# Self-attention over four images in exact-split fp32: biases as one row, later images' projection in pairs of units

## Chip, cores and metric

The kernel runs on one core of a Trainium2 chip. The metric is device time in microseconds (us) of one launch. Each engine of the core runs its own queue in order: PE (TensorE; its weight loads are shown as PEld), ACT (ScalarE), DVE (VectorE), POOL (GpSimd) and SP (SyncE, which here only issues DMAs).

## The reference

Input x has shape (4, 64, 64, 256). Per image (N = 4096 positions, C = 256):

```python
q = x @ Wq + bq                 # (N, 128)
k = x @ Wk + bk                 # (N, 128)
v = x @ Wv + bv                 # (N, 256)
pq, pk, pv = q.reshape(128, N), k.reshape(128, N), v.reshape(256, N)
energy = pq.T @ pk              # (N, N)
attention = softmax(energy, axis=-1)
out = gamma * (pv @ attention.T) + x
```

The reshapes reinterpret memory, they do not transpose.

## The kernel before, in words

**Split arithmetic.** A value y is carried as three "forms" in the fp32r format: h (most of y), l (the rest, y - h) and d (h and l mixed with other weights). A product of two values is then three matmul passes (form numbers f = 0, 1, 2). ACT writes h; DVE writes l and d, each from y and h. `split` (L151) does this for x and v, `qk_forms` (L261) for q and k, `upper` (L341, ACT) and `halves` (L348, DVE) for the exponentials. With `two` set, `split` lets DVE write l and POOL write d (L159).

**Work units.** Projection of an image is cut into 16 units of 256 positions. A unit is: load x (`load_x`, SP), four PE transposes into a PSUM bank (`transposed`, L214), the three forms of x (`x_forms`), q and k by 8 + 4 matmuls of 256 columns (`products` with w = 0, L239), v by as many (w = 1); a bias added in PSUM between the first pass and the others (`seed_qk` on DVE, `seed_v` on ACT); forms of q, k and v, and stores of these to DRAM by SP (`store`, L292). Image 0 is projected first, in a phase of its own (about the first 70 us), with v's forms written straight into `vall` in SBUF. Images 1 to 3 are projected while the image before them is attended; their v comes back through DRAM (`load_v`, POOL).

**Attention.** There are 512 steps n (128 an image). A step handles 256 keys (t = n mod 16) for 512 queries; 16 steps are a group. In a step PE does, in this order: `cross(n+2)`, 2 matmuls (form 2 of k and q; ACT then scales the PSUM tile e, L322); `attend(n, 0)`, 6 matmuls of 512 columns for the first 128 channels: 2 with h and 2 with l into bank a0, 2 with d into b0; `energy(n+2)`, 4 matmuls onto e, after which ACT takes exp (L339); a piece of projection; and `attend(n, 1)`, 6 matmuls for the other channels (banks a1, b1). That is 18 matmuls of 512 columns. ACT's `upper(n+2)` writes h of the new exponentials. DVE's `halves(n+1)` adds them to the running sum (L356), then writes l (L370) and d (L372).

**The turn.** After step t = 15 the four banks a0, b0, a1, b1 are full. ACT empties a0 and b0 in step t = 15 and a1, b1 in the next step (t = 0) after its exp (`emptied`, L407), which `attend(n, 1)` of step t = 0 waits for; `upper` of the step is put off behind that. ACT also writes zf, h of the group's total (`sum_forms`, L419; DVE writes its l), which PE sums over partitions in step t = 0 (`sums`, z, L431); ACT copies z out (L432), and `finish`, one piece a step, sends 1/z around through DRAM and stores the output.

**Order.** The schedule is manual: each engine runs its instructions in the order in which the Python code emits them, and tiles of one tag share a ring of buffers, so a new tile waits until the last user of its buffer is done. `step(p, engine)` (L522) emits the projection's piece number p on one engine: unit p // 8, stage r = p mod 8. In the loop (L646) p = n - 4 up to n = 15, two pieces a step for n = 16 to 23, then p = n + 4. Two PSUM banks, p0 and p1, are used in turn for x transposed, q and k, v, and z. In image 3's steps (`late`) no projection is left, and a1 and b1 are emptied in step t = 1.

**Biases.** bq and bk are loaded with one copy for each of the 128 partitions (L131, L132), bv into two columns by POOL (L128); ACT and POOL scale them (L588, L587).

## Time and profile before

| | |
|---|---|
| median of 3 runs | 2358.5 us (2358.07 to 2359.53) |
| profiled execution | 2360.35 us, its span 2358.6 us |
| DMA | 413.82 MB, mean 175 GB/s |
| ACT's 128 x 512 emptying (L407) | 0.69 to 0.70 us each, 124 of them |
| DVE 128 x 1024 (L356, L370, L372) | 1.22 us each, 480 of each |
| DVE 128 x 512 form of q, k (L271), x and v (L163) | 0.68 us each |
| v store (vf) of a unit, k load | 768 KB by SP, 384 KB by POOL (3.7 us to landing) |

The span runs from the first to the last instruction. Busy time of PE is modelled from pipelined matmuls, so the distance between starts says more than a duration. In a waits line stand the engine and line that waited, what released it, the total in us, how often, and the longest. In a timeline stand the start, the duration, engine, line, operation, output<-inputs, shapes, a count, and in brackets idle time before and its releaser.

### The profile page before, as it was taken

How to read it: one execution, taken by the hardware profiler on the slowest of the kernel's cores; microseconds unless marked ns; L12 is line 12 of the kernel's file. 1: busy time of each engine (PE TensorE's matmuls, PEld its weight loads, DVE VectorE, ACT ScalarE, POOL GpSimd, SP SyncE). 2: the span in 40 equal slices, each digit the busy share in tenths (PEclk: the TensorE clock that was granted, in tenths of full speed). 3: DMA queues.
4: the chain of work that ended last, by engine and by line, in shares of the span. 5: the costliest groups of instructions: out<-in, count | busy, mean ns of one | idle time of the engine just before them, and what ended most of it. 6: DMA issues, size and time to landing. Idle time of an engine off the chain costs nothing.

```text
span 2358.6 us, 31984 instructions
## 1 busy us (share of the span) xinstructions
PE 2340.2 (99%) x11104; PEld 1955.8 (83%) x11104; DVE 2129.4 (90%) x2095; ACT 1870.8 (79%) x3074; POOL 397.7 (17%) x671
## 2 busy tenths in 40 slices
PE   8999999999999999999999999999999999999998
PEld 8888888888888888888888888888888888888886
DVE  7989999989999899998999999999989888888887
ACT  6778778888788887888877888778887777888875
POOL 6211111111211111111121111111112111111110
PEclk9999999999999999999999999999999999999999
DMA  8556665556975566556597555665559554454443
GB/s 259 175 157 171 186 165 165 164 158 178 295 247 175 148 172 186 159 162 157 165 340 226 159 167 152 184 169 162 168 154 353 158 135 120 123 130 117 131 130 96
DMA packets 179110, 413.82 MB, mean 175 GB/s; under 512 B 26079, under 2 KB 76767, under 8 KB 178942
## 3 DMA queue, kind: packets, MB, share of 16 engines
q0 software_dynamic: 94208, 280.54, 45.2%
q1 hardware_dynamic: 83902, 130.77, 15.5%
q8 instruction: 91, 1.49, 0.3%
q14 instruction: 77, 0.63, 0.1%
q10 hardware_dynamic: 832, 0.39, 0.1%
HBM read 306.64 MB, written 104.98 MB: 175 GB/s over the span
## 4 chain that ended last, share of the span: by engine, by line
PE 96%; ACT 1%; DVE 1%; POOL 1%; issue 0%; DMA 0%; SPq 0%; DVEq 0%; ACTq 0%; POOLq 0%
PE a L393 39%; PE e L336 20%; PE b L393 19%; PE e L321 10%; PE qv L239 7%; PE xt L214 1%; PE z L431 1%; ACT x L339 0%; ACT o L407 0%; DMA xs<-in_x_dram 0%; POOL xf L159 0%; ACT e L322 0%; POOL v L159 0%; DVE f L271 0%; DVE ld L372 0%
## 5 line engine op out<-in xcount | busy, mean ns | idle before, releaser
L339 ACT ACTIVATE x<-e 128x512 f32<-128x512 f32 x960 | 522.3, 596 | 296.6 <-PE e L336 290.3
L356 DVE TENSOR_TENSOR s<-s,x 128x1024 f32<-128x1024 f32 x480 | 586.3, 1222 | 94.1 <-ACT x L339 91.5
L370 DVE TENSOR_TENSOR ld<-x,h 128x1024 fp32r<-128x1024 f32 x480 | 585.9, 1221 | 88.2 <-ACT h L345 57.9
L393 PE MATMUL a<-h,v 128*128 128x512 f32 x2048 | 641.0, 394 | 0.0
L393 PE MATMUL b<-ld,v 128*128 128x512 f32 x2048 | 631.6, 390 | 1.7 <-DVE ld L372 1.7
L322 ACT ACTIVATE e<-e 128x512 f32<-128x512 f32 x1024 | 546.7, 572 | 108.9 <-PE e L321 108.6
L393 PE MATMUL a<-ld,v 128*128 128x512 f32 x2048 | 632.7, 390 | 0.0
L308 POOL DMA_DIRECT2D k<-kf x512 | 272.7, 533 | 1903.4 <-PE e L336 1797.5
L372 DVE SCALAR_TENSOR_TENSOR ld<-h,x 128x1024 fp32r<-128x1024 f32 x480 | 585.6, 1220 | 0.0
L336 PE MATMUL e<-q,k 128*128 128x512 f32 x2048 | 548.8, 390 | 1.1
L345 ACT ACTIVATE h<-x 128x1024 fp32r<-128x1024 f32 x480 | 510.3, 1063 | 13.3
L393 PEld LDWEIGHTS b<-ld,v 128*128 128x128 f32 x2048 | 384.2, 188 | 84.7 <-DVE ld L372 1.5
L393 PEld LDWEIGHTS a<-ld,v 128*128 128x128 f32 x2048 | 384.5, 188 | 83.1
L336 PEld LDWEIGHTS e<-q,k 128*128 128x128 f32 x2048 | 383.1, 188 | 84.4 <-ACT e L322 6.0
L393 PEld LDWEIGHTS a<-h,v 128*128 128x128 f32 x2048 | 368.6, 189 | 69.4 <-ACT o L407 7.3
L321 PE MATMUL e<-q,k 128*128 128x512 f32 x1024 | 316.0, 390 | 0.0
L321 PEld LDWEIGHTS e<-q,k 128*128 128x128 f32 x1024 | 191.8, 188 | 40.7 <-issue 0.2
L239 PEld LDWEIGHTS qv<-wf,xf 128*128 128x128 f32 x768 | 107.5, 192 | 10.4 <-POOL xf L159 1.3
L239 PE MATMUL qv<-wf,xf 128*128 128x256 f32 x768 | 112.9, 286 | 1.8 <-DVE xf L163 0.8
L239 PEld LDWEIGHTS qv<-xf,wf 128*128 128x128 f32 x768 | 106.3, 191 | 8.8 <-ACT s L432 0.7
L239 PE MATMUL qv<-xf,wf 128*128 128x256 f32 x768 | 110.5, 283 | 0.5 <-ACT s L432 0.3
L271 DVE SCALAR_TENSOR_TENSOR f<-f,qv 128x512 fp32r<-128x512 f32 x128 | 85.7, 680 | 3.6 <-ACT f L268 2.1
(78 smaller groups left out, 1021.6 us busy)
## 6 DMA issues: line engine op xcount, KB each, us to landing
k<-kf POOLq DMA_DIRECT2D x512, 384.0 KB, 3.7
vf<-vf SPq DMA_DIRECT2D x48, 768.0 KB
v<-vf POOLq DMA_DIRECT2D x48, 768.0 KB, 7.8
kf<-f SPq DMA_DIRECT2D x128, 192.0 KB
qd<-f SPq DMA_DIRECT2D x128, 192.0 KB
q<-qd POOLq DMA_DIRECT2D x31, 768.0 KB, 4.7
o<-in_x_dram POOLq DMA_DIRECT2D x31, 512.0 KB, 7.3
out_dram<-o SPq DMA_DIRECT2D x31, 512.0 KB
```

What stands on the lines that cost most here:

```text
L239: nc.tensor.matmul(to[:, s, :], left, right.rearrange("p s a -> p (s a)") if w else right, start=(f == 2 and s == k == 0), stop=(f == 1 an ...
L271: nc.vector.scalar_tensor_tensor(f[:, :, :, j, :], h.bitcast(F32), s, y, ALU.mult, op)
L308: nc.gpsimd.dma_start(t, kf[b, u % NU])
L321: nc.tensor.matmul(e, *forms(n, i, 2), start=True, stop=False, skip_group_check=True)
L322: nc.scalar.mul(e, e, -REST)
L336: nc.tensor.matmul(e, *forms(n, i, f), start=False, stop=(f == 1), skip_group_check=True)
L339: nc.scalar.activation(x[:, i, :], e, AF.Exp, scale=(1.0 + E) ** 3 / E)
L345: nc.scalar.activation(h, units[n], AF.Identity, scale=UPPER)
L356: nc.vector.tensor_tensor(s, s, x, ALU.add)
L370: nc.vector.tensor_tensor(l, x, h.bitcast(F32), ALU.subtract)
L372: nc.vector.scalar_tensor_tensor(d, h.bitcast(F32), 1.0 + E, x, ALU.mult, ALU.subtract)
L393: nc.tensor.matmul(to, vall[:, t, f, i, j * P : (j + 1) * P], units[n][f][:, i, :], start=(t == 0 and i == 0 and f != 1), stop=(t == NU - ...
```

## The change

- **Biases.** bq, bk and bv are loaded as one row of 512 on one partition, on ACT's queue. PE spreads bq and bk over the partitions (a matmul of a column of ones with the row) and turns bv into two columns (two matmuls with a single 1); ACT scales from PSUM.
- **Image 0.** Unit 1's forms are all DVE's; unit 2 is transposed later, after v of unit 0 has begun. v's forms of units 14 and 15 are DVE's alone.
- **Later images by pairs.** A piece sequence now has 16 stages for two units. Both units are transposed together; x's forms h and l lie side by side for both units, d in the buffer in which x was loaded (tag "xd"). q and k stay 256 columns wide. v is made for both units at once by 512-column matmuls, one half of the channels at a time (`products_v`), with one seed for each half. A half's forms go to DRAM in two stores. `vall` and vf have the order half, form instead of form, half.
- **One step behind.** p = n - 3 + (n > 6) + (n > 17), with two pieces in steps 6 and 17 alone; from n = 18 on stage 15, which emits nothing, falls on t = 0.
- **Turn.** In steps t = 0 (not in image 3) `attend(n+1, 0)` with h and l is emitted ahead of `attend(n, 1)`; in t = 1 only its d is left between `cross` and `energy`.
- **Buffers.** zf takes a buffer of the ring "pf" (the forms of q, k and v, two buffers); the row of 1/z goes into the second half of o.

```diff
-        vall = qkv.tile([P, NU, 3, 2, C], F32R, tag="v", name="v")
+        vall = qkv.tile([P, NU, 2, 3, C], F32R, tag="v", name="v")
...
-        nc.scalar.dma_start(bias[:, :C2], bq.partition_broadcast(P))
-        nc.scalar.dma_start(bias[:, C2:], bk.partition_broadcast(P))
+        nc.scalar.dma_start(rows[:, :C2], bq.unsqueeze(0))
+        nc.scalar.dma_start(rows[:, C2:C], bk.unsqueeze(0))
+        nc.scalar.dma_start(rows[:, C:], bv.unsqueeze(0))
...
+            pair = work.tile([P, 2, 2, XB], F32, tag="xd", name=f"x_{b}_{i}", bufs=1)
+            for u in range(2):
+                nc.sync.dma_start(pair[:, u], xv[b, i + u])
+                loads["x", b, i + u] = pair[:, u]
...
-            yield from split(f[:, 0], f[:, 1], f[:, 2], y, b == 0 and i > 0)
+            yield from split(*f, y, b == 0 and i > 1)
...
+        def products_v(b, i, eh, fs):
+
+            xf = now["xf"]
+            if fs[0] == 2:
+                units["v", b, i, eh] = bank(f"v{eh}_{b}_{i}", [P, 2, C], b, 1)
+            to = units["v", b, i, eh]
+            for f in fs:
+                for k in range(KC):
+                    nc.tensor.matmul(
+                        to.rearrange("p u c -> p (u c)"),
+                        wf[:, 1, f, k, eh * P : (eh + 1) * P],
+                        xf[f][:, k].rearrange("p u s a -> p (u s a)"),
...
+        def seed_v_pair(b, i, eh):
+            y = units["v", b, i, eh]
+            nc.scalar.activation(y, y, AF.Identity, bias=bvs[:, eh : eh + 1], scale=REST)
...
+            yield from split(*(vall[:, i, :, f] for f in range(3)), y, i < NI - 2)
+
+        def v_pair_forms(b, i, eh):
+            y = units.pop(("v", b, i, eh))
+            f = work.tile([P, 2, 3, C], F32R, tag="pf", name=f"vf{eh}_{b}_{i}")
+            yield from split(*(f[:, :, j] for j in range(3)), y)
+            for u in range(2):
+                stores.append((vf[b, i + u][:, eh], f[:, u]))
...
-            f = work.tile([P, 2, NB], F32R, tag="r", name=f"zf_{n // NU}", bufs=1)
+            f = work.tile([P, 2, NB], F32R, tag="pf", name=f"zf_{n // NU}")
...
-            r = work.tile([P, NB], F32, tag="r", name=f"r_{n}", bufs=1)
+            r = o[:, 1, 0]
...
+            if engine == "pe":
                 if r == 0:
                     transposed(b, i)
+                    transposed(b, i + 1)
+                elif r == 5:
                     products(b, i, 0, (2,))
+                    products(b, i + 1, 0, (2,))
+                elif r == 6:
                     products(b, i, 0, (0, 1))
+                    products(b, i + 1, 0, (0, 1))
+                elif r in (9, 11):
+                    products_v(b, i, r // 11, (2,))
+                elif r in (10, 12):
+                    products_v(b, i, r // 12, (0, 1))
+            elif engine == "act":
+                if r in (1, 2):
+                    begin(("x", r - 1), x_forms(b, i + r - 1))
+                elif r in (7, 8):
+                    begin(("qk", r - 7), qk_forms(b, i + r - 7))
+                elif r in (10, 12):
+                    seed_v_pair(b, i, r // 12)
+                    if r == 12:
+                        load_x(b + (i + 2) // NI, (i + 2) % NI)
+                elif r in (11, 13):
+                    begin(("v", r // 13), v_pair_forms(b, i, r // 13))
+            else:
+                if 1 <= r <= 4:
+                    next(made["x", (r - 1) // 2])
                 elif r == 5:
+                    seed_qk(b, i)
+                    seed_qk(b, i + 1)
+                elif 7 <= r <= 10:
+                    next(made["qk", (r - 7) // 2])
...
+                elif 11 <= r <= 14:
+                    next(made["v", (r - 11) // 2])
...
-            p = n - 4 if n < 16 else 2 * n - 20 if n < 24 else n + 4
+            p = n - 3 + (n > 6) + (n > 17)
             step(p, "act")
-            if not final:
+            late = n >= (B - 1) * STEPS
+            if t == 1 and n > 1 and not late:
+                attend(n, 0, (2,))
+            elif not final:
                 attend(n, 0)
...
+            if t == 0 and n and not late:
+                attend(n + 1, 0, (0, 1))
             attend(n, 1)
...
-            if 16 <= n < 24:
+            if n in (6, 17):
                 for engine in ("act", "pe", "dve"):
                     step(p + 1, engine)
```

More of the change, by code (lines that the diff above doesn't have):

```diff
@@ L126 @@
         nc.gpsimd.memset(zs, 1.0)
-        for eh in range(KC):
-            nc.gpsimd.dma_start(bvs[:, eh : eh + 1], bv[eh * P : (eh + 1) * P].unsqueeze(1))
+        rows = work.tile([P, 2, XB], F32, tag="pf", name="rows")[:1]
+        rows = rows.rearrange("p s f -> p (s f)")
         make_identity(nc, ident)
         nc.vector.tensor_scalar(ones_r, zs.to_broadcast([P, P]), 1.0, None, ALU.mult)
-        nc.scalar.dma_start(bias[:, :C2], bq.partition_broadcast(P))
-        nc.scalar.dma_start(bias[:, C2:], bk.partition_broadcast(P))
+        nc.scalar.dma_start(rows[:, :C2], bq.unsqueeze(0))
+        nc.scalar.dma_start(rows[:, C2:C], bk.unsqueeze(0))
+        nc.scalar.dma_start(rows[:, C:], bv.unsqueeze(0))
         nc.scalar.activation(zs, zs, AF.Exp)
@@ L183, in image @@
                 kf[b, t] = dram.tile([P, 2, 3, P], F32, tag=f"kf{t}", name=f"kf_{b}_{t}")
-                vf[b, t] = dram.tile([P, 3, 2, C], F32, tag=f"vf{t}", name=f"vf_{b}_{t}")
+                vf[b, t] = dram.tile([P, 2, 3, C], F32, tag=f"vf{t}", name=f"vf_{b}_{t}")
         def bank(name, shape, b, ring):
@@ L198, in load_x @@
         def load_x(b, i):
-            if i >= NI:
+            if b == B or i >= NI:
                 return
@@ L202, in load_x @@
                 t = xs4[:, i % 4]
-            else:
-                t = work.tile([P, 2, XB], F32, tag="xin", name=f"x_{b}_{i}", bufs=1)
-            if b or i:
-                nc.sync.dma_start(t, xv[b, i])
-            loads["x", b, i] = t
+                if i:
+                    nc.sync.dma_start(t, xv[b, i])
+                loads["x", b, i] = t
+                return
+            pair = work.tile([P, 2, 2, XB], F32, tag="xd", name=f"x_{b}_{i}", bufs=1)
+            for u in range(2):
+                nc.sync.dma_start(pair[:, u], xv[b, i + u])
+                loads["x", b, i + u] = pair[:, u]
         def transposed(b, i):
@@ L218, in x_forms @@
             y = units.pop(("xt", b, i))
-            if b == 0 and i % 3 < 2:
-                f = ppool.tile([P, 3, KC, 2, P], F32R, tag="ld", name=f"xf_{b}_{i}")
-            else:
-                f = work.tile([P, 3, KC, 2, P], F32R, tag="xf", name=f"xf_{b}_{i}", bufs=1)
+            if b == 0:
+                if i % 3 < 2:
+                    f = ppool.tile([P, 3, KC, 2, P], F32R, tag="ld", name=f"xf_{b}_{i}")
+                else:
+                    f = work.tile([P, 4, KC, 2, P], F32R, tag="xf", name=f"xf_{b}_{i}", bufs=1)
+                f = [f[:, j] for j in range(3)]
+            else:
+                if i % 2 == 0:
+                    shape = [P, 2, KC, 2, 2, P]
+                    f = work.tile(shape, F32R, tag="xf", name=f"xf_{b}_{i}", bufs=1)
+                    d = work.tile([P, *shape[2:]], F32R, tag="xd", name=f"xd_{b}_{i}", bufs=1)
+                    now["xf"] = [f[:, 0], f[:, 1], d]
+                f = [y_[:, :, i % 2] for y_ in now["xf"]]
             units["xf", b, i] = f
-            yield from split(f[:, 0], f[:, 1], f[:, 2], y, b == 0 and i > 0)
+            yield from split(*f, y, b == 0 and i > 1)
         def products(b, i, w, fs):
@@ L235, in products @@
                         if w:
-                            left, right = wf[:, 1, f, k, s * P : (s + 1) * P], xf[:, f, k]
+                            left, right = wf[:, 1, f, k, s * P : (s + 1) * P], xf[f][:, k]
                         else:
-                            left, right = xf[:, f, k, s, :], wf[:, 0, f, k]
+                            left, right = xf[f][:, k, s, :], wf[:, 0, f, k]
                         nc.tensor.matmul(
@@ L246, in products @@
                         )
+        def products_v(b, i, eh, fs):
[9 more added lines that the diff above has]
+                        xf[f][:, k].rearrange("p u s a -> p (u s a)"),
+                        start=(f == 2 and k == 0),
+                        stop=(f == 1 and k == KC - 1),
+                        skip_group_check=True,
+                    )
         def seed_qk(b, i):
@@ L252, in seed_qk, with seed_v @@
             )
-        def seed_v(b, i):
-            y = units[1, b, i]
+        def seed_v(i):
+            y = units[1, 0, i]
             for eh in range(KC):
@@ L277, in qk_forms, with v_forms @@
                 stores.append((qd[b, i // NJ + NG // 2 * s][:, i % NJ], f[:, s, 0]))
-        def v_forms(b, i):
-            y = units.pop((1, b, i))
-            units.pop(("xf", b, i))
-            if b == 0:
-                f = vall[:, i]
-            else:
-                f = work.tile([P, 3, 2, C], F32R, tag="pf", name=f"vf_{b}_{i}")
-            yield from split(f[:, 0], f[:, 1], f[:, 2], y, b == 0)
-            if b:
-                stores.append((vf[b, i], f))
+        def v_forms(i):
+            y = units.pop((1, 0, i))
+            units.pop(("xf", 0, i))
+            yield from split(*(vall[:, i, :, f] for f in range(3)), y, i < NI - 2)
[5 more added lines that the diff above has]
+                stores.append((vf[b, i + u][:, eh], f[:, u]))
         def store():
@@ L394, in attend @@
                         to,
-                        vall[:, t, f, i, j * P : (j + 1) * P],
+                        vall[:, t, i, f, j * P : (j + 1) * P],
                         units[n][f][:, i, :],
@@ L471, in finish_last @@
             S = now["sum"][:, 0, :]
-            f = work.tile([P, 2, NB], F32R, tag="r", name="zf_last", bufs=1)
+            f = work.tile([P, 2, NB], F32R, tag="pf", name="zf_last")
             nc.scalar.activation(f[:, 0, :], S, AF.Identity, scale=UPPER)
@@ L517, in finish_last @@
             nc.sync.dma_start(og[b, g][:, 1], xr[:, 1, :])
-        R = STEPS // NI
+        R = 2 * STEPS // NI
         def step(n, engine):
@@ L527, in step, with begin @@
             i, r = divmod(u, R)
-            b += 1
+            b, i = b + 1, 2 * i
+            if b >= B:
+                return
             made = now["made"]
-            if engine == "pe" and b < B:
+            def begin(key, pieces):
+                made[key] = pieces
+                next(pieces)
+            if engine == "pe":
                 if r == 0:
                     transposed(b, i)
-                elif r == 3:
+                    transposed(b, i + 1)
+                elif r == 5:
@@ L534, in step @@
                     products(b, i, 0, (2,))
-                elif r == 4:
+                    products(b, i + 1, 0, (2,))
+                elif r == 6:
                     products(b, i, 0, (0, 1))
-                elif r == 5:
-                    products(b, i, 1, (2,))
-                elif r == 6:
-                    products(b, i, 1, (0, 1))
-            elif engine == "act" and b < B:
-                if r == 1:
-                    made["x"] = x_forms(b, i)
-                    next(made["x"])
-                    load_x(b, i + 1)
-                elif r == 5:
-                    made["qk"] = qk_forms(b, i)
-                    next(made["qk"])
-                elif r == 6:
-                    seed_v(b, i)
-                elif r == 7:
-                    made["v"] = v_forms(b, i)
-                    next(made["v"])
-            elif engine == "dve":
-                if r == 0 and "v" in made:
-                    for _ in made.pop("v"):
-                        pass
-                if b < B:
-                    if r in (1, 2):
-                        next(made["x"])
-                    elif r == 3:
-                        seed_qk(b, i)
-                    elif r == 5:
-                        next(made["qk"])
-                    elif r == 6:
-                        for _ in made.pop("qk"):
-                            pass
-                    elif r == 7:
-                        next(made["v"])
@@ new lines, in step @@
+                    products(b, i + 1, 0, (0, 1))
[14 more added lines that the diff above has]
+                    begin(("v", r // 13), v_pair_forms(b, i, r // 13))
+            else:
+                if 1 <= r <= 4:
+                    next(made["x", (r - 1) // 2])
+                elif r == 5:
+                    seed_qk(b, i)
+                    seed_qk(b, i + 1)
+                elif 7 <= r <= 10:
+                    next(made["qk", (r - 7) // 2])
+                    if r % 2 == 0:
+                        next(made["qk", (r - 7) // 2], None)
+                elif 11 <= r <= 14:
+                    next(made["v", (r - 11) // 2])
+                    if r % 2 == 0:
+                        next(made["v", (r - 11) // 2], None)
@@ L586 @@
         next(w0)
-        nc.gpsimd.tensor_scalar(bvs, bvs, REST / E, None, ALU.mult)
-        nc.scalar.activation(bias, bias, AF.Identity, scale=REST)
         next(w1)
         products(0, 0, 0, (2,))
+        bb = ps_e.tile([P, KC + C], F32, tag="e", name="bb")
+        nc.tensor.matmul(bb[:, KC:], ones[:1], rows[:, :C], start=True, stop=True)
+        nc.scalar.activation(bias, bb[:, KC:], AF.Identity, scale=REST)
         seed_qk(0, 0)
-        xs = []
-        for i in (1, 2):
-            transposed(0, i)
-            load_x(0, i + 3)
-            xs.append(x_forms(0, i))
-            next(xs[-1])
-        next(xs[0])
+        transposed(0, 1)
+        load_x(0, 4)
+        x1 = x_forms(0, 1)
+        next(x1)
         next(w1)
+        next(x1)
         next(w1)
+        next(x1)
         nc.gpsimd.tensor_scalar(gam1, gam, 1.0 + E, None, ALU.mult)
@@ L607 @@
             if i == 0:
-                products(0, 0, 1, (2,))
-                seed_v(0, 0)
+                for eh in range(KC):
+                    nc.tensor.matmul(
+                        bb[:, eh : eh + 1],
+                        rows[:, C + eh * P : C + (eh + 1) * P],
+                        ones[:1, :1],
+                        start=True,
+                        stop=True,
+                    )
+                nc.scalar.activation(bvs, bb[:, :KC], AF.Identity, scale=REST / E)
+                products(0, 0, 1, (2,))
+                seed_v(0)
+                transposed(0, 2)
+                load_x(0, 5)
+                x2 = x_forms(0, 2)
+                next(x2)
             if i + 1 < NI:
@@ L616 @@
             if i == 0:
-                next(xs[1])
+                next(x2)
             products(0, i, 1, (0, 1))
-            vs = v_forms(0, i)
+            vs = v_forms(i)
             next(vs)
@@ L624 @@
                 products(0, i + 1, 1, (2,))
-                seed_v(0, i + 1)
+                seed_v(i + 1)
             if i + 3 < NI:
@@ L654 @@
                 image(b + 2)
-                load_x(b + 2, 0)
             if n == B * STEPS - 6:
@@ L672 @@
             store()
-            late = n >= (B - 1) * STEPS
             if t == 0 and n:
```

## The prediction

> **What bounds the kernel now.** I read the page first, then the chain that ended last, the waits, and the timeline of single steps. TensorE (PE) is the bound:

> ```profile
> PE 2340.2 (99%) x11104; PEld 1955.8 (83%) x11104; DVE 2129.4 (90%) x2095; ACT 1870.8 (79%) x3074; POOL 397.7 (17%) x671
> ...
> PE 96%; ACT 1%; DVE 1%; POOL 1%; issue 0%; DMA 0%; SPq 0%; DVEq 0%; ACTq 0%; POOLq 0%
> ```

> Busy 99% does not yet say that PE streams without gaps, so I look at spacing. The chain in order of time shows the first matmuls after each group turn (a group is 16 steps; a turn is a step with t = 0):

> ```profile
> 660.54 1.08 PE a L393 x4
> ...
> 733.34 1.08 PE a L393 x4
> ```

> A group takes 72.80 us, and so does every later group that carries projection, to 0.01 us. PE's timeline gives the prices inside it:

> ```profile
> 700.72 0.64 PE L239 MATMUL qv<-xf,wf 128*128 128x256 f32 x4
> 701.20 0.63 PE L393 MATMUL a<-h,v 128*128 128x512 f32 x2
> ...
> 705.30 1.11 PE L239 MATMUL qv<-xf,wf 128*128 128x256 f32 x8
> 706.25 0.63 PE L393 MATMUL a<-h,v 128*128 128x512 f32 x2
> ...
> 714.45 0.60 PE L214 MATMUL xt<-ident,x 128*128 128x128 f32 x4
> ```

> Starts, not durations, are the price. A 512-column matmul follows the last after 0.2269 us, a 256-column one after 0.120 us, a transpose after 0.108 us. Every small block also makes the next few 512-column matmuls a little late; with that a block of four costs 0.498, of eight 0.978, four transposes 0.477 (blocks measured to the eighth matmul behind them). One unit of projection is 0.477 + 2 x 0.498 + 2 x 0.978 = 3.43. A group: 290 x 0.2269 (16 steps of 18 matmuls, and z) + 2 x 3.43 = 72.66. What is left, 0.16, is the turn.

> **Pairs, and v 512 columns wide.** Per pair of units PE now does 8 transposes in a row (0.477 + 4 x 0.108 = 0.909), q and k as a block of 8 and one of 16 (0.978 + 1.938), and v as 12 matmuls of 512 columns in place of 24 of 256 (12 x 0.2269 = 2.723, no small block among the others). Sum 6.548 against 6.856: 0.308 saved, 24 pairs: **-7.4 us**, bounds -8 and -1.1 (the transposes' 0.045 alone). ACT and DVE do the same splits (DVE 0.68 each, starting 0.61 apart); v's seed is two ACT passes of about 0.6 a pair instead of four of 0.45, on an engine with 21% idle. DVE's heaviest step carries 3 x 1.155 + 0.61 + 1.15 = 5.2 us against PE's 4.08, but the steps around it are light, and before had peaks as high without making PE wait.

> [...]

> **The turn.** This is the step that I fear. The waits, then the turn at 729.04 (call it T), PE, ACT and DVE:

> ```profile
> PEld a L393 <- ACT o L407: 7.3, 23, 0.3
> ```
> ```profile
> 729.04 0.62 PE L321 MATMUL e<-q,k 128*128 128x512 f32 x2
> ...
> 731.76 1.12 PE L239 MATMUL qv<-wf,xf 128*128 128x256 f32 x8
> 732.71 0.63 PE L431 MATMUL z<-zf,ones 128*128 128x512 f32 x2
> 733.22 0.73 PE L393 MATMUL a<-h,v 128*128 128x512 f32 x2
> ```
> ```profile
> 729.46 1.07 ACT L322 ACTIVATE e<-e 128x512 f32<-128x512 f32 x2 [0.30 <-PE e L321]
> 730.43 1.06 ACT L345 ACTIVATE h<-x 128x1024 fp32r<-128x1024 f32 x1
> ...
> 734.57 0.56 ACT L432 COPY s<-z 1x512 f32<-1x512 f32 x1
> 735.13 1.07 ACT L322 ACTIVATE e<-e 128x512 f32<-128x512 f32 x2
> ```
> ```profile
> 731.53 1.23 DVE L370 TENSOR_TENSOR ld<-x,h 128x1024 fp32r<-128x1024 f32 x1 [1.78 <-ACT h L345]
> ```

> From T on ACT has no idle until the next step's e. PE waited 0.16 at 733.22 for ACT to empty a's bank, and the block of eight (0.98) covered the rest. In the changed kernel the projection stands one step behind, so the step with t = 0 has no block; z, then h and l of the next step's attend(n+1, 0), stand there instead. Step by step, from T, with the same durations:
> - PE would reach l of step n+1 at 2.72 (energy done) + 0.454 (z) + 0.454 (h) = T + 3.63. DVE ends that l at 731.53 + 1.23, T + 3.72; the step before the turn is shorter now (4.08, not 4.58, no block), so ACT's e starts at T + 0.49 instead of 0.42, and l ends at 3.78. A wait that ends late costs its weight load too: at 733.22 the second matmul came 0.34 after the first, not 0.23, and the load started 0.05 after ACT's end. So l runs from 3.78 + 0.16 = 3.94: 0.31 lost.
> - Then l, attend(n, 1): next step at T' = 3.94 + 0.454 + 1.361 = 5.755. a's bank (free at about 4.2) is no longer waited for.
> - There only d stands between cross and energy, 0.907 after T' instead of 1.81. ACT's e starts at 6.17 by its own chain and by cross (T' + 0.42) alike, and the first ends at 6.76: energy runs from 6.92, not 6.66, and its second half loses 0.04 more.
> The whole loses 0.61 a turn, where before lost 0.16: 0.45 x 23 turns = **+10.4 us**. Bounds: -3.7 (nothing waits) and +17 (ACT's chain 0.3 later still).

> **zf in the ring of the forms ("pf").** At each turn ACT writes zf into the buffer of the pair's first v half, so it waits for that half's two stores, and exp, emptying and e stand behind it on ACT. DVE finishes that half some 3.1 us into step t = 13, SP issues at once, behind the next pair's two loads of x. ACT wants zf 10.5 us into step 13 (4.99 + 4.08 + 1.46), 7.4 us after the issue. The packets of an ordinary vf store of before ended 5.7 us after their issue: in time, with 0.38 us of idle on ACT behind. But in the last group of an image v is loaded too (DMA share 1.0 to 1.1 from 608 to 657 us), and the stores at 642.9, 1225.4 and 1807.5 ended after 10.6, 9.6 and 7.0 us. By these ACT is late by 3.2, 2.2 and 0, less 0.38 each: 4.7 us for three turns; by the ordinary row 0. I take the middle, **+2.3**, bounds 0 and +10 (two smaller stores in place of one, behind more loads). The 48 further store issues (0.55 us each) cost SP nothing, it is mostly idle. POOL's loads of the last v pair wait a little longer for their stores; the k loads behind them have three steps, 12 us, of lead over a landing of 3.7.

> **Image 0's end.** v's d of units 14 and 15 moves from POOL to DVE:

> ```profile
> 70.61 2.31 DVE L372 SCALAR_TENSOR_TENSOR ld<-h,s 128x1024 fp32r<-128x1024 f32 x1
> ```
> ```profile
> 69.64 2.20 POOL L159 TENSOR_TENSOR v<-v 128x512 fp32r<-128x512 f32 x1 [1.49 <-DVE v L156]
> ```

> Side by side both run nearly twice as long as alone (DVE 1.22, POOL 1.3). It comes again at 75.8, and PE waits for this DVE row both times (1.1 and 0.9 us). Without POOL, DVE saves 1.09 and pays 0.61 each time: **-0.9**, bounds -1 and +1.2 (if POOL is not the cause).

> **Double steps.** Before runs two projection steps in each of 16 to 23; at 148.0 PE lost 0.57 there to the copy of z. The changed kernel doubles only 6 and 17: **-0.6**, or 0.

> **The start.** PE stands from 7.6 to 10.55 for the second x; ACT's bias waits until 10.43 for a broadcast row, 128 KB with its partner. One row of 2 KB and a small matmul in PE's idle time take their place; x_1 lands earlier by up to 1 us, the first q and k no longer stand behind unit 2's transposes, and POOL loses a pass, but DVE gets x_1's d and the next wait (POOL until 20.03) is fed by DVE. PE's granted clock is 0.5 between 9.1 and 15.9 us, so nothing is made up there. **-1.0**, bounds -2 and +1 (late rows hold PE's queue). Image 3 has no projection and is unchanged.

> **Sum.** -7.4 + 10.4 + 2.3 - 0.9 - 0.6 - 1.0 = +2.8 us. The profiled execution took 2360.35 (span 2358.6), so it would take 2363.2; the median of the runs is 1.85 lower, 2358.5, and gives **2361.3**. A measurement here can tell about 0.2%, 4.7 us, from no change: 2353.8 to 2363.2 is "the same".

> **Rivals.**
> - *The turn's waits vanish* (faster): l and e come early enough and the 0.16 goes as well: -3.7 in place of +10.4, 2347.2. For it: 0.31 and 0.30 are small against chains of ten instructions. Against: ACT's chain has no gap to give. It decides where l ends before T + 3.47.
> - *zf holds ACT at every turn* (slower): if the two stores take 9 us in ordinary groups as well, 1.2 lost x 20 turns, 2385; with 8.2 us, 0.4 each, 2369. For it: x's loads stand ahead. Against: 5.7 us was steady.
> - *v's pairs save nothing*: if a wide v matmul costs as much as two of 0.120, and switching as much as before, only the transposes' 0.045 a pair is left, -1.1 in place of -7.4: 2367.6. Against: 0.120 and 0.2269 repeat in all groups. [...]

> **How the numbers follow.** Forecast 0.48, range of its own 2355 to 2367: of it 0.03 falls under "faster", 0.33 "same", 0.12 "slower". Waits vanish 0.22, all faster. zf 0.16: 0.03 same, 0.13 slower. No saving 0.06, slower. Small terms at their other bounds 0.08: 0.01, 0.05, 0.02. Faster 0.26, same 0.41, slower 0.33. The range, 2347 to 2371, takes in the first rival and the small end of the second.

> **What would show it.** Right: a group of about 73 us between z's; among the waits PEld for DVE's ld and for ACT's e, some 23 each, and none for ACT o until image 3; DVE's row at 70.6 back at 1.22; v matmuls 0.227 apart. Wrong: groups under 72.4, or zf waiting for vf's DMA outside three turns.

## The result and the profile after

Before took 2358.96 us (median of 6 runs, 2358.07 to 2359.53), the changed kernel 2378.26 us (6 runs, 2373.45 to 2382.86): ratio 1.0081, 95% interval 1.0070 to 1.0092. It is 0.8% slower, and lies 7 us above the top of the range on record. Its profiled execution took 2377.93 us (span 2376.0).

The page of the changed kernel: first the busy times, then the shares of the chain that ended last.

```profile
PE 2353.1 (99%) x10822; PEld 1943.2 (82%) x10822; DVE 2127.3 (90%) x2098; ACT 1853.7 (78%) x3027; POOL 389.4 (16%) x665
...
PE 89%; ACT 5%; DMA 2%; DVE 2%; issue 1%; SPq 0%; POOL 0%; ACTq 0%; DVEq 0%
```

PE is still "busy" for 99%, but the chain tells another story: before, PE alone made 96% of it; now 89%, and DMA holds 2% where it held 0%. DMA on the chain means that somebody on the critical path waits for a transfer. The waits name who (engine and line, what it waited for: us in total, times, longest):

```profile
PEld e L371 <- ACT e L357: 19.9, 62, 0.6
...
PEld a L428 <- DVE ld L405: 10.5, 21, 0.7
PEld e L356 <- ACT x L374: 9.9, 8, 4.2
ACT zf L454 <- DMA vf<-vf: 8.3, 3, 4.8
ACT vf L154 <- DMA qd<-f: 8.2, 5, 2.8
PE e L356 <- ACT x L374: 7.1, 4, 3.8
...
ACT vf L154 <- DMA vf<-vf: 2.1, 1, 2.1
...
PEld a L428 <- ACT o L442: 1.3, 4, 0.4
```

Two families. The small and frequent ones (0.7 and 0.6 at most) are the turn: l and e arrive late, as forecast (of the 62 waits for e, two at each of 23 turns are new; the other 16 stand in image 3, where before has them too). The wait for ACT's emptying of o has shrunk from 23 times to 4, at 146.2, 661.3, 1251.2 and 1838.9 us, each behind one of the large waits. The large and rare ones are new: ACT waits 3 times for a store of v's forms before it may write zf, 5 times for stores of q and k and once for one of v's before it may write a v half, and PE then waits for ACT's exp (x), up to 4.2 us at a time.

The chain in order of time over one ordinary turn shows the first family as a row of pieces:

```profile
733.60 1.09 ACT x L374 x2
734.69 1.16 ACT o L442 x2
735.85 0.97 ACT e L357 x2
736.81 0.98 ACT h L380
737.80 0.02 issue
737.82 1.24 DVE ld L405
739.06 0.04 issue
739.10 1.65 PE a L428 x6
```

ACT makes exp, empties two banks, makes e and h without a pause, DVE makes l, and PE's `a<-ld` starts 0.04 after l's end. Where did the time come from? I measured from z to z (the matmul that sums zf, once in each group), one interval for each group:

```
z to z, us   ordinary groups   last group of image 0   of image 1   the group with image 2's end
before       72.80 to 72.81    72.81                   72.81        79.46
after        72.86 to 72.99    78.29                   79.81        83.53
```

Nineteen ordinary intervals grew by 0.17 each on average, 3.2 us together (seventeen of them take 72.97 to 72.99; the two that follow the long groups 72.94 and 72.86). Two groups grew by 5.5 and 7.0, the third by 4.1 (the third holds more work after than before, see v_not_loaded below). These three, in which v of the next image is loaded, and the first turn are the story. This is ACT and PE in the first of them, changed kernel (start and duration in us, engine, line, what, and in brackets the idle time before it and who ended it):

```profile
643.34 0.60 ACT L154 ACTIVATE vf<-v 128x512 fp32r<-128x512 f32 x1 [2.55 <-DMA qd<-f]
...
659.07 0.63 ACT L454 ACTIVATE zf<-s 128x512 fp32r<-128x512 f32 x1 [3.35 <-DMA vf<-vf]
```
```profile
657.72 0.61 PE L428 MATMUL b<-ld,v 128*128 128x512 f32 x2
660.24 0.98 PE L356 MATMUL e<-q,k 128*128 128x512 f32 x2 [1.91 <-ACT x L374]
661.31 0.73 PE L428 MATMUL a<-h,v 128*128 128x512 f32 x2
661.88 0.77 PE L428 MATMUL a<-ld,v 128*128 128x512 f32 x2
662.44 1.05 PE L428 MATMUL b<-ld,v 128*128 128x512 f32 x2
663.29 1.91 PE L371 MATMUL e<-q,k 128*128 128x512 f32 x4
```

ACT stands 3.35 us at zf; exp stands behind zf, cross behind exp, and PE loses 2.07 at once and 0.61 in the next starts (a "stand" of PE, below, is time that it loses like this to a wait). Then comes something that the prediction had no term for: the block of four at 663.29 takes 1.91 instead of 1.07. The busy times by stretch say why (columns: the stretch, its length, busy time of PE, PEld, DVE, ACT and POOL, then the granted clock, the busy share of the DMA engines, and GB/s):

```profile
640.00:658.00 18.00, 17.51 (x76) 13.61 (x74) 13.76 (x14) 11.71 (x20) 3.86 (x8) 1.00 1.10 400
658.20:660.20 2.00, 0.14 (x1) 0.00 (x0) 0.47 (x1) 1.13 (x3) 0.17 (x1) 1.00 1.07 346
662.20:665.60 3.40, 3.40 (x10) 2.62 (x9) 1.79 (x2) 2.53 (x5) 0.10 (x1) 0.50 0.73 288
665.70:669.00 3.30, 3.30 (x15) 2.46 (x14) 2.27 (x3) 3.19 (x7) 0.86 (x2) 1.00 0.71 211
```

The DMA share is 1.1 while the stores are awaited, PE does next to nothing for 2 us, and behind that the clock is 0.5 for 3.4 us, in which each matmul starts 0.43 after the last. In the next image's last group the stand is 3.91 and the half clock lasts 6.8 us (1249.31 to 1256.14).

### The profile page after: what moved, and what is told of

The parts are those of the page before. It is cut to its first block, busy times and chain, and to the rows that moved or that the text cites. A ratio compares the mean times of both kernels' runs of the same rounds, so it can differ in the third digit from the quotient of the medians.

```text
span 2376.0 us, 31544 instructions
## 1 busy us (share of the span) xinstructions
PE 2353.1 (99%) x10822; PEld 1943.2 (82%) x10822; DVE 2127.3 (90%) x2098; ACT 1853.7 (78%) x3027; POOL 389.4 (16%) x665
## 3 DMA queue, kind: packets, MB, share of 16 engines
q8 instruction: 89, 1.46, 0.3%
## 4 chain that ended last, share of the span: by engine, by line
PE 89%; ACT 5%; DMA 2%; DVE 2%; issue 1%; SPq 0%; POOL 0%; ACTq 0%; DVEq 0%
PE a L428 36%; PE e L371 18%; PE b L428 18%; PE e L356 9%; PE qv L252 5%; PE v L269 2%; ACT x L374 2%; ACT o L442 1%; DVE ld L405 1%; PE xt L218 1%; DMA vf<-vf 1%; DMA qd<-f 1%; ACT e L357 1%; ACT h L380 1%; DVE ld L407 0%
## 5 line engine op out<-in xcount | busy, mean ns | idle before, releaser
L407 DVE SCALAR_TENSOR_TENSOR ld<-h,x 128x1024 fp32r<-128x1024 f32 x480 | 585.8, 1220 | 0.0
L428 PEld LDWEIGHTS a<-ld,v 128*128 128x128 f32 x2048 | 383.0, 188 | 89.9 <-DVE ld L405 10.5
L428 PEld LDWEIGHTS a<-h,v 128*128 128x128 f32 x2048 | 379.6, 188 | 76.1 <-ACT o L442 1.3
L252 PE MATMUL qv<-wf,xf 128*128 128x256 f32 x576 | 79.2, 289 | 1.7 <-POOL xf L160 0.8
L252 PEld LDWEIGHTS qv<-wf,xf 128*128 128x128 f32 x576 | 75.4, 195 | 5.1 <-POOL xf L160 1.0
L164 DVE SCALAR_TENSOR_TENSOR vf<-vf,v 128x512 fp32r<-128x512 f32 x96 | 65.4, 682 | 5.9 <-ACT vf L154 5.8
L405 DVE TENSOR_TENSOR ld<-s,h 128x1024 fp32r<-128x1024 f32 x32 | 39.2, 1226 | 29.7 <-ACT h L380 28.2
```

The costliest lines, as they stand in the source:

```text
L252: nc.tensor.matmul(to[:, s, :], left, right.rearrange("p s a -> p (s a)") if w else right, start=(f == 2 and s == k == 0), stop=(f == 1 an ...
L405: nc.vector.tensor_tensor(l, x, h.bitcast(F32), ALU.subtract)
L407: nc.vector.scalar_tensor_tensor(d, h.bitcast(F32), 1.0 + E, x, ALU.mult, ALU.subtract)
L428: nc.tensor.matmul(to, vall[:, t, i, f, j * P : (j + 1) * P], units[n][f][:, i, :], start=(t == 0 and i == 0 and f != 1), stop=(t == NU - ...
```

## Experiments

The theory: the excess lies in the ring "pf". It has two buffers; in the changed kernel they hold q's and k's forms, both v halves and zf. In the last group of an image the v loads make the stores long, ACT waits in its order for a buffer, PE for ACT, and the granted clock falls behind a long stand. The rivals: the loads themselves make PE wait; the new order of the turn costs more than it hides; the start.

**zf_in_xf** (changed kernel, zf in a ring that is free at that time):

```diff
-            f = work.tile([P, 2, NB], F32R, tag="pf", name=f"zf_{n // NU}")
+            f = work.tile([P, 2, NB], F32R, tag="xf", name=f"zf_{n // NU}", bufs=1)
```

> The changed kernel with one edit: zf is written into the ring of x's forms (free between the pair's last v matmul and the next pair's x_forms), not into the ring pf. Theory (ACT stands at zf, in the last group of each image, for a vf store that the v loads slow down, and the stall is made dearer by half clock behind it): no ACT wait at zf is left; the group of 78.29 us falls to about 74.0 (the v half's wait of 0.65 and its followers stay), that of 79.81 to 73 to 74, that of 83.53 hardly moves (its loss stands at v halves that wait for qk stores), the first turn gets 1.9 back; no half clock at 662 and 1249. Total about 2365 (2363 to 2368). Rival (the DMA load makes PE itself wait, for v or k, wherever zf is written): the three groups stay within 1 us of 78.3, 79.8 and 83.5, total 2376 to 2378.

Measured: 2364.57 us (10 runs, 2361.25 to 2366.17), against 2359.73 of before (25 runs), ratio 1.0018 (1.0008 to 1.0028). The group of 78.29 fell to 74.03, that of 79.81 to 72.97, the wait at the first turn is gone, ACT waits for no DMA at zf any more, and the clock does not fall at 662 and 1249. The third group was a miss: it rose from 83.53 to 85.61. There a v half waited longer for stores of q and k, and another half clock followed:

```profile
1810.41 0.60 ACT L154 ACTIVATE vf<-v 128x512 fp32r<-128x512 f32 x1 [4.30 <-DMA qd<-f]
```
```profile
1790.00:1808.00 18.00, 18.00 (x81) 14.90 (x80) 16.09 (x16) 13.16 (x21) 5.62 (x10) 1.00 0.99 309
...
1811.30:1814.70 3.40, 3.15 (x7) 2.46 (x8) 3.11 (x4) 3.29 (x6) 0.00 (x0) 0.50 1.13 417
```

So one edit of a tag takes back about 14 of the 19 us: with the loads unchanged, one of the three groups has no excess left and another 1.05 us, behind a v half that waits 2.43. What PE waited for was the buffer, not the loads themselves. The v halves' place in the same ring stays a second source; no run takes it out alone, and why the third group waited longer here is not shown.

**v_not_loaded** (changed kernel without the loads of v for images 1 to 3, which work on image 0's v):

```diff
-            if n >= STEPS - NU + 3 and (n - 3) // NU % NG == NG - 1 and (n - 3) // STEPS + 1 < B:
-                load_v((n - 3) // STEPS + 1, (n - 3) % NU)
```

> The changed kernel without the loads of v for images 1 to 3 (they work on image 0's v; this part of the computation is changed). Theory (ring wait made long by the v loads): the three groups 78.29, 79.81 and 83.53 fall to 73.0, 73.0 and 79.5 or a little less, zf waits nowhere but at the first turn (2.06 us of ACT, which is a store one step old and has no v load beside it); total about 2378.3 - 16.6 = 2361.7 (2360 to 2364). Rival (stores are slow because of their own number and size, not of the loads): zf's waits stay and the total is 2372 or more. A fall well below 2360 would say that v loads also cost something in the kernel before.

Measured: 2362.41 us (10 runs, 2359.86 to 2364.80). The first two groups are 72.98 and 72.98, and of ACT's waits for stores of some length one is left, at the first turn:

```profile
ACT vf L154 <- DMA vf<-vf: 2.2, 1, 2.2
```

The third group is 81.58, not 79.5: I had taken all of its excess over before for waiting, and about half of it, 2.12, is left without the v loads. It is projection that the changed kernel does here and the kernel before did earlier: in this interval the traces have a whole pair after the change (24 matmuls of 256 columns, 12 of 512, 8 transposes), and 36 matmuls of 256 columns and 4 transposes before, 1.7 us less at their starts' distances; the first interval of before is 76.84, that of the changed kernel 73.20. The rest, 0.4, is the turn. So the waits of the third group are worth 83.53 - 81.58 = 1.95, not 4.1. With zf_in_xf this says that in the last groups of images 0 and 1 both the near ring and the loads are needed: take either away and most of the standing goes. At the first turn the ring alone is enough, since the store there is only a step old.

**turn_undone** (changed kernel, attend in the order of before):

```diff
-            if t == 1 and n > 1 and not late:
-                attend(n, 0, (2,))
-            elif not final:
+            if not final:
                 attend(n, 0)
...
-            if t == 0 and n and not late:
-                attend(n + 1, 0, (0, 1))
             attend(n, 1)
```

> The changed kernel with attend in the order of before at each turn (no h and l of the next step's first half pulled ahead). Theory: the step with t = 0 has no projection block, so PE waits for the emptying of a's bank with nothing to cover it: 0.16 as before plus the 0.98 of the block that is gone, about 1.1 us a turn in place of 0.59; group 73.5, total 2378.3 + 0.5 x 23 = 2390 (2384 to 2394), PEld a <- ACT o back among the waits with some 20 waits. Rival (the reordering is what costs the 0.59 and hides nothing): group 72.4 to 72.6, total 2365 to 2370.

Measured: 2388.99 us (4 runs, 2388.19 to 2390.96). Ordinary groups take 73.42 against 72.98. The turn on PE:

```profile
741.09 1.08 PE L371 MATMUL e<-q,k 128*128 128x512 f32 x4
742.00 0.63 PE L466 MATMUL z<-zf,ones 128*128 128x512 f32 x2
743.46 0.72 PE L428 MATMUL a<-h,v 128*128 128x512 f32 x2 [0.82 <-ACT o L442]
```

From the start of z to that of a 1.46 where 0.454 is the work: 1.0 lost, and 0.1 in the matmul behind it. The new order is the better one of the two, and the rival that the order is the cost falls. The run also prices the pairs by themselves: 73.42 less 1.09 is 72.33, and the prediction's 65.80 + 6.548 is 72.35.

**image0_end** (kernel before, only the end of image 0 changed):

```diff
-            yield from split(f[:, 0], f[:, 1], f[:, 2], y, b == 0)
+            yield from split(f[:, 0], f[:, 1], f[:, 2], y, b == 0 and i < NI - 2)
```

> The kernel before with only the end of image 0 changed: d of v's last two units made by DVE, not POOL. Theory: DVE's row at 70.6 falls from 2.31 to 1.22 us, PE gets 0.9 us back (0.7 to 1.2), total 2357.6 to 2358.2 where before is 2358.9. Rival (POOL was not the cause of the slow DVE rows): they stay at 2.3 and the total is 2358.9 to 2360.

Measured: 2358.79 us (10 runs) against 2359.73 (25 runs), ratio 0.9997, interval 0.9987 to 1.0006: the times can't tell it from nothing. The trace can. DVE, first row at the place of the 2.31 of before:

```profile
70.86 1.22 DVE L372 SCALAR_TENSOR_TENSOR ld<-h,s 128x1024 fp32r<-128x1024 f32 x1
```

From the first attend to the first z, before, start_only and stalls, all with the old end, take 75.21, 75.22 and 75.21 us, and this run 74.24: 0.97 gained. POOL was the cause: DVE's row takes 2.31 beside POOL's of 2.20, and 1.22 when that one is DVE's own work. Why the one row lengthens the other is not shown.

**start_only** (kernel before with only the start changed):

```diff
-        nc.scalar.dma_start(bias[:, :C2], bq.partition_broadcast(P))
-        nc.scalar.dma_start(bias[:, C2:], bk.partition_broadcast(P))
+        nc.scalar.dma_start(rows[:, :C2], bq.unsqueeze(0))
+        nc.scalar.dma_start(rows[:, C2:C], bk.unsqueeze(0))
+        nc.scalar.dma_start(rows[:, C:], bv.unsqueeze(0))
...
+        bb = ps_e.tile([P, KC + C], F32, tag="e", name="bb")
+        nc.tensor.matmul(bb[:, KC:], ones[:1], rows[:, :C], start=True, stop=True)
+        nc.scalar.activation(bias, bb[:, KC:], AF.Identity, scale=REST)
```

> The kernel before with only the start changed: biases as one row that PE spreads, transposes of units 1 and 2 apart, x_1's d by DVE. Theory (what the prediction said): 1.0 us less, 2357.9 against 2358.9, first attend at 69.7 to 70.0 us where two profiles without the change have 70.7 and 71.0. Rival (the half clock and the two-pass bias matmuls in PE's order eat the gain, as the profile after suggests, where PE came out of the start 0.5 us later): no change or up to 0.5 us more, first attend at 70.8 to 71.5.

Measured: 2359.49 us (11 runs, 2356.78 to 2360.66) against 2359.77 (15 runs), ratio 0.9998, interval 0.9988 to 1.0007. A gain of 1.0 is neither seen nor excluded. The traces don't settle it either: the first attend starts at 71.03, 70.68 and 70.14 in three profiles with the old start, and anywhere from 67.96 to 71.34 in six with the new. The start's half clock does not end at one time: it ends at 15.9 us in before and at 17.1 in the profile after, and the mean granted clock of the first 30 us is 0.89 in before, start_only and zf_in_xf and 0.94 in qk_at_turn. That is not all that varies: with 0.89 in all three, before has 71.03, start_only 70.75 and zf_in_xf, with the same new start, 69.98.

**stalls** (kernel before, with further copies of z on ACT at twelve turns, which make PE stand):

```diff
-            nc.scalar.copy(now["total"][0:1, 0, :], zp[0:1, :])
+            for _ in range(1 + STALL.get(n // NU, 0)):
+                nc.scalar.copy(now["total"][0:1, 0, :], zp[0:1, :])
```

> The kernel before, with 1, 2, 3, 4, 6 and 8 further ACT copies of z (the same row again, some 0.5 us each) behind the copy of z in the turns after groups 2 to 7, and the same again after groups 10, 11, 12, 13, 14 and 16: PE is made to stand for about 0.2, 0.7, 1.1, 1.6, 2.5 and 3.5 us, away from any v load except behind group 7. Theory (a stand of PE of 2 us and more is followed by some us of half granted clock, whatever caused it): the groups with 6 and 8 copies are longer than 72.80 by the stand and by 1.5 to 3 us more, with 0.5 in the granted clock behind them; those with 1 to 3 copies by the stand alone. Rival (half clock at 662 and 1249 came with the v loads, not with the stand): every group is longer by its stand alone and the clock stays at 1.0.

Measured: 2385.76 us (one execution). A single further copy cost nothing. The stands of 0.34, 0.95 and 1.56 us (twice each) made their groups 0.47, 1.08 and 1.70 longer, the same both times, at full clock. Of two stands of about 2.77, one made its group 4.48 longer and the other 2.92; of two of 3.98, 5.65 and 6.79. PE behind the two stands of about 2.77, the first and the second (in brackets the part of the stand in which no matmul ran):

```profile
596.04 1.70 PE L336 MATMUL e<-q,k 128*128 128x512 f32 x4 [2.60 <-ACT e L322]
```
```profile
1191.87 1.20 PE L336 MATMUL e<-q,k 128*128 128x512 f32 x4 [2.61 <-ACT e L322]
```

The theory holds for the first (half clock from 596.50 to 599.91) and not for the second, at whose end the clock stays at 1.00. How the two differ is in the last section. The rival, that the v loads bring the half clock, falls: the turns at 593 and 1337 have none.

**qk_at_turn** (changed kernel; old order of the turn, projection six steps ahead, z in the ring of e):

```diff
-            p = n - 3 + (n > 6) + (n > 17)
+            doubled = (6, 8, 10, 12, 14, 18, 20, 22, 24)
+            p = n - 3 + sum(n > m for m in doubled)
...
-                zp = spare(f"z_{n // NU}", [P, NB])
+                zp = ps_e.tile([P, NB], F32, tag="e", name=f"z_{n // NU}")
```

> The changed kernel with three edits: attend in the order of before at the turns; the projection six steps ahead (nine steps doubled in the first two groups), so that q's and k's block of 16 matmuls, 1.94 us of PE, stands in the step with t = 0 and zf's buffer was last used eight steps earlier; z in the ring of e, since both other banks hold q and k then, and its copy ahead of the upper half of x. Theory (pairs are worth 0.308 a group; a block of PE's own work covers the emptying of the banks; zf's stalls came from the near ring): group 65.80 + 6.548 = 72.35 plus at most 0.16, no zf wait for a DMA, last groups of images within 1.5 us of the others, total 2358.9 - 0.4 x 22 - 1.1 = 2349 (2346 to 2353), faster than the kernel before. Rival (something else in the pairs costs, ACT's forms beside the turn or z in e's ring): group 72.8 or more, total 2358 or more.

Measured: 2349.77 us (5 runs, 2347.90 to 2350.67) against 2358.99 (9 runs), ratio 0.9962 (0.9949 to 0.9976): faster than both kernels. Its chain, and its turn on PE and on ACT:

```profile
PE 96%; ACT 2%; DMA 1%; DVE 1%; issue 0%; SPq 0%; POOL 0%; ACTq 0%; DVEq 0%
```
```profile
728.40 2.08 PE L252 MATMUL qv<-wf,xf 128*128 128x256 f32 x16
730.31 0.63 PE L466 MATMUL z<-zf,ones 128*128 128x512 f32 x2
730.77 0.62 PE L428 MATMUL a<-h,v 128*128 128x512 f32 x2
```
```profile
729.68 0.70 ACT L442 ACTIVATE o<-b,gam 128x512 f32<-128x512 f32 x1
```

ACT ends the emptying of o at 730.38; PE, with 1.91 us of q and k in front, asks for the bank at 730.77. Nothing waits, and ordinary groups take 72.25, 0.55 less than before. zf is still in "pf", but that buffer was stored eight steps earlier: no wait for a DMA stands at zf, and the last groups of images 0 and 1 take 73.33 and 72.25 (PE waits there once, 0.81 us at 636.02, for a load of k). Being in the ring is not what costs; being close in it is.

## Why the prediction was wrong

Step by step, from what moved the time least to what moved it most:

- **Pairs and turn: right.** A group was to take 65.80 + 6.548 + 0.61 = 72.96, and takes 72.98. At the turn l was to end at T + 3.78 and energy to run from T + 6.92; with T = 735.22 (cross, 2.72 ahead of z at 737.94) DVE ends l at 739.06, T + 3.84, and energy starts at 742.10, T + 6.88. v's wide matmuls follow each other after 0.227 (four from 788.24, the next block at 789.15), as the sum had them. turn_undone shows pairs and turn apart. One sign was off: waits for ACT's o come at three turns before image 3, not at none, each of them behind a large wait.
- **Double steps: right.** The 0.57 lost at 148.0 in before is not in the profile of zf_in_xf.
- **Image 0's end: right**, 0.97 by the trace of image0_end where 0.9 was said.
- **The start: not shown.** Said -1.0; the profile after has its first attend 0.3 later than before's, start_only is 0.3 us under before with 2 us of uncertainty, and single executions vary by more. It stays open, and is small either way.
- **zf in the ring: the mis-sized term, +2.3 (bounds 0 and +10) where the stands cost 16.** This is the step that failed: what ACT's waits in the ring "pf" cost PE. In pieces, from the trace after: at zf in the last groups of images 0 and 1, PE lost 2.68 and 3.91, 6.6 together. The price by the rows of the slow stores, 4.7, was already too low, since the stores ended 9.4, 12.1 and 8.7 us behind their issue and not 10.6, 9.6 and 7.0; with these the prediction's own working gives 6.9. And I took the middle between 4.7 and 0, although the trace of before had shown that in just these groups the stores are slow. The row that belongs to the place was the one to take. (In the other groups of the changed kernel the stores of the first half ended 4.5 to 6.4 us behind their issue, so the rival that zf holds ACT at every turn did not come.) Three more pieces had no term at all:
  - the v halves wait in the same ring for the stores of q and k (ACT 8.2 us over 5 waits; PE 0.91 in the first of the three groups and, by the difference to v_not_loaded, 1.95 in the third, of which the trace has 1.64 at 1833.95). I had priced the ring for zf alone;
  - at the first turn the projection stands at another phase, the second v half takes the first one's buffer a step after its store was issued, and PE loses 1.87. I had read the ring only in the steady phase;
  - half clock behind the two longest stands, both at zf. It lasted 3.41 and 6.83 us; its price is no measurement of its own but what is left of the 5.31 and 6.83 us that the two groups took beyond 72.98: 1.7 and 2.9 us.

  Sum: 2.68 + 3.91 + 0.91 + 1.95 + 1.87 + 4.6 = 15.9. zf alone, with the half clock behind it, is 11.2 of it and above the term's upper bound.

The sum on record, +2.8, with 15.9 in place of 2.3 and 0 in place of the start's -1.0, is 17.4; the profiled executions differ by 17.6 (2377.93 and 2360.35). Since two of the pieces are remainders (the half clock's 4.6 and the 1.95), this agreement bears out the other terms and not the price of the half clock. The medians differ by 19.3, and single runs of the changed kernel by up to 9 among themselves, where before's differ by 1.5: how long the stands are hangs on when the transfers land, most likely, but only one of these runs has a trace. That zf would wait for vf's DMA was also among my signs of failure "outside three turns": it waits in three, and the chain behind it is what I had too small.

## What to carry to other kernels

When a tile moves into a shared ring, list every writer of the ring in order, in each phase of the schedule, and price the wait of each against the slowest transfer seen at that place; an average over quiet places is no forecast for the busy one. Distance in the ring, in steps between the store and the next use, is what to design for: the same ring with zf eight steps behind its predecessor cost nothing. And a block of the bound engine's own work, put where that engine would wait, can hide the wait fully: with 16 matmuls of projection at the turn an ordinary group takes 72.25 where it took 72.98. The two together turned a change that lost 19 us into one that gains 9.

## What the runs showed of the hardware

For steps of the grid I added up the time that PE lost beyond its normal spacing, by stands and by slower starts:

```
trace    step of the grid, us   PE lost, us   clock in it   clock in the next
after     143.40 to  146.81     1.87          1.00          1.00
after     658.81 to  662.22     2.15          1.00          0.50
after     662.22 to  665.63     1.5           0.50          1.00
after    1245.90 to 1249.31     3.1           1.00          0.50
after    1249.31 to 1252.73     2.2           0.50          0.50
after    1252.73 to 1256.14     1.6           0.50          1.00
stalls    593.09 to  596.50     2.77          1.00          0.50
stalls   1187.0  to 1190.4      1.32          1.00          1.00
stalls   1190.4  to 1193.8      1.56          1.00          1.00
```

In the step that ended at 662.22 PE stood for 2.15 of 3.41 us and worked for the rest, and the clock fell all the same. The stand of 2.77 in stalls that fell across two steps of the grid (parted at 1190.4) was free of half clock, and the one of the same length inside one step made its group 4.48 longer and not 2.92, 1.6 more. These are nine steps of two traces: the most that full clock followed is 1.87, the least that half clock followed is 2.15, and none of the nine lies between the two.
